# Weights of layers 2 to 4 turned on VectorE from 32-column blocks, and the first gates in a new order

## The chip, the cores and the metric

The kernel runs on one core of a Trainium2 chip. The metric is the device time of one execution in microseconds (us); shown is the median of the runs. Beside it there is one profiled execution with a trace. The engines are named as the profile names them: PE is TensorE (PEld its weight loads), DVE is VectorE, ACT is ScalarE, POOL is GpSimd, and SP is SyncE, which here only issues DMA transfers. A small q behind a name (SPq) is the engine's sequencer.

## The reference

Sixteen graphs of 1024 nodes with 128 features each. `x` is (16, 1024, 128), `adj` is (16, 1024, 1024) with entries 0 and 1. Two networks run one after the other, each on the layer norm of its input and with a residual.

```python
# first network: four layers of a gated graph network, h = relu(layernorm(x))
for i in range(4):
    hw = h @ weight[i]
    m = einsum('bjn,bjd->bnd', adj, hw)            # adj transposed
    gx, gh = m @ w_ih[i].T + b_ih[i], h @ w_hh[i].T + b_hh[i]
    r, z = sigmoid(xr + hr), sigmoid(xz + hz)      # thirds of gx and gh
    n = tanh(xn + r * hn)
    h = (1 - z) * n + z * h
x = x + h * mask
# second network: four layers of a graph convolution, h = relu(layernorm(x))
for i in range(4):
    h = relu(adj @ (h @ W[i]) + b[i])
    h = gamma[i] * (h - mean) * rsqrt(var + 1e-5) + beta[i]   # over all graphs and nodes
x = x + h
```

## The kernel before

The work is laid out by features across nodes: a hidden state is a tile of 128 features by 1024 nodes, in two halves of 512. The kernel uses `exact_path`; `general_path` stands behind a flag for other inputs and is not run here.

**First network.** Two graphs go at once, as two streams, `sa` (even graphs, A) and `sb` (odd graphs, B). A half step (`half_step(one, two)`, L1090) does the gates of stream `two` on ScalarE and VectorE while TensorE does the aggregation of stream `one`. An aggregation (`aggregate_rows`, L518) takes the features as a high and a low part (`hw[0]`, `hw[1]`) and one rounded row block of the adjacency after the other: four products of 128x512 for each of eight rows. `products` (L992) then makes the four gate sums of a half with six full f32 products. `w_mT` holds weight and w_ih multiplied together, so that `m` doesn't need its own weight product; `join_layer` (L484) makes it out of turned weights.

The order of all engines in this part is written out by hand (`tc.manual_schedule`): each engine runs its instructions as the program text lists them. An `agenda` (`at`, `due`) puts extra work at named places of a half step.

Each half of a new state goes out to DRAM and comes back with other strides (`half_out` or `turned_half` turn it in 32x32 blocks on VectorE, `exchange_out` L603 writes it, `exchange_in` L609 reads it with four transfers); all of these are issued by SP. What comes back is copied into the high part by ScalarE (`high`, L932, L937) and into the low part by VectorE (`low`, L939, L944).

**Start.** Before the loop of half steps, the first layer of graphs 0 and 1 is written out by hand (L1154 to L1282). TensorE turns the weights of layer 0 with transposes (`turn_hh`, `turn_ih`), ScalarE copies them out of PSUM, idle transposes (L1158) fill the wait for x. `first_rows` loads row blocks of the adjacency, `first_round` rounds them on GpSimd or ScalarE. Looks and glances (`first_look` on VectorE, `first_glance` on ScalarE) scan rows for values that are not exact. The order of the layer's end for A and the begin for B is:

```python
            exchange_in(out0, half_of(sa.y, 0))
            sa.candidate(1)
            ...
            out1 = turned_half(sa.new, sa.y, 1, "h0_1")
            exchange_in(out1, half_of(sa.y, 1))
```

The weights of layers 1 to 3 (in the program's count, which starts at 0; layers 2 to 4 in the title) are loaded by `load_layer` with one transfer each and turned by TensorE as well, at gaps of the aggregation. That is 21 transposes of 128x128, with copies on ScalarE.

**Second network.** Sixteen graphs times four layers of aggregation and product, ordered by the tile framework. **Tail.** After the last layer each graph's 1024 nodes are scaled (L1656 to L1662, tile `bn`), turned back by TensorE (L1667, `pt_o`), added to x by VectorE (L1669) and stored by SP (L1671 by pieces, L1673 for a whole graph); `whole` (L1508) says which.

Of the kernel before, what the change touches and what calls it, by code (L numbers as in the profile page):

```python
# [8 lines left out]
F32 = mybir.dt.float32  # L9
# [332 lines left out]
def exact_path(  # L342
# [115 lines left out]
    def load_layer(i):  # L458

        for src, nm in ((g_w_hh, "hh"), (g_w_ih, "ih")):  # L460
            wn = half_tile(f"wn_{nm}{i}").bitcast(F32)[:, : 3 * C].rearrange("p (g c) -> p g c", c=C)
            nc.sync.dma_start(wn, src[i].rearrange("(g p) c -> p g c", p=P))
            wns[nm, i] = wn
# [10 lines left out]
    def turn_ih(prep, w_g, i):  # L474
# [4 lines left out]
        nc.tensor.transpose(pt[:, 3 * P :], w_g[:, i, :], ident)  # L479
        both = prep.tile([P, 4 * C], F32, tag="w_both", name=f"w_both{i}", bufs=1)  # L480
# [50 lines left out]
    with ExitStack() as st:  # L531
# [138 lines left out]
        def norm_scale(nt, k0, k1):  # L670
            norm_invert(nt, k0, k1)
            rs, ms = (t[:, k0:k1, 0] for t in nt[2:])
            nc.vector.scalar_tensor_tensor(ms, nt[1][:, k0:k1, 0], -1.0, rs, ALU.mult, ALU.mult)
# [71 lines left out]
        class Stream:  # L745
# [231 lines left out]

            def open_reset(self):
                nc.tensor.matmul(self.opened[0], w_hhT[:, 0, :C], self.hT[:, :HALF], start=True, stop=False)

# [11 lines left out]
            def products(self, hf):  # L992
# [18 lines left out]
                if self.opened:  # L1011
                    part(pz, w_hhT, 1, hin, True, False)
# [77 lines left out]
        def half_step(one, two, gated=None, halfway=None, rest=None):  # L1090
# [32 lines left out]
            one.low(1)  # L1123
            two.candidate(1)
# [15 lines left out]
            if halfway:  # L1140
                halfway()
            one.agg_step(1)
            if rest:
                rest()
# [6 lines left out]
        with tc.manual_schedule(engines=every):  # L1151
# [8 lines left out]
            idle(20)  # L1160
# [3 lines left out]
            for k0, eng in ((0, nc.sync), (BH, nc.scalar)):  # L1164
                x0_d = x[0].rearrange("(k p) c -> p k c", p=P)[:, k0 : k0 + BH, :]
                eng.dma_start(x0[:, k0 : k0 + BH, :], x0_d)
            small_in = load_small(prep)
            load_layer(0)
            w_g = flat("w_g")[:, :L, :]
# [6 lines left out]
            first_rows(0, range(NB), raw0)  # L1176
            x1 = load_x(1, nc.sync)
            halves = [[half_tile(f"early{j}_{k}").bitcast(F32) for k in range(2)] for j in range(3)]
# [10 lines left out]
            sa.sums(range(4, 5))  # L1189
# [3 lines left out]
            turn_ih(prep, w_g, 0)  # L1193
            sa.centred_high(0)
            turn_half(sa.y, "in0", h0, 0, AF.Relu)
            sa.sums(range(5, 7))
            join_layer(0)
            pt = acc("g_xn", "pt_idle1")
            idle(6)
            sa.centred_low(0)  # L1200
            sa.sums(range(7, NB))
# [3 lines left out]
            sa.centred_high(1)  # L1205
            sa.centred_low(1)
            for j in range(4):
                sa.rows[j] = first_round(0, j, raw0[j], nc.gpsimd)
            sa.hT = h0
            sa.agg_rows(range(1))  # L1210
            sa.open_gates()
            sa.agg_rows(range(1, 4))
            sa.open_reset()
            for j in range(2):
# [3 lines left out]
            first_look(0, 2, raw0[2])  # L1218
            sa.agg_rows(range(4, 6))
            for j, eng in ((6, nc.scalar), (7, nc.gpsimd)):  # L1220
                sa.rows[j] = first_round(0, j, raw0[j], eng)
            turn_half(sa.y, "in0", h0, 1, AF.Relu)
            turn_small(*small_in)
            sa.agg_rows(range(6, NB))

            sb.sums(range(NB))
            sb.rows[0] = first_round(1, 0, raw1[0], nc.scalar)
            norm_root(sb.norm, 0, NB)
            norm_scale(sb.norm, 0, NB)
            first_look(0, 3, raw0[3])  # L1230
            first_rows(1, range(4, NB), quarters)
            for j in range(1, NB):
                sb.rows[j] = first_round(1, j, raw1[j], nc.gpsimd)

            load_layer(1)
            nc.sync.dma_start(w_g[:, 1:, :], w_d[:, 1:, :])
            nc.gpsimd.dma_start(w_c, c_w.rearrange("l c d -> c l d"))
            sb.hT, sb.across = h1, True

            def half_of(t, hf):  # L1240
                return t[:, hf * HALF : (hf + 1) * HALF]

            def beside(hf):
                sb.normed(range(hf * BH, (hf + 1) * BH))
                sb.split_high(hf)
                sb.split_low(hf)
# [6 lines left out]
            sa.products(0)  # L1253
            sa.reset_gate(0)
            sa.update_gate(0)
            beside(0)
            in0 = turned_half(sb.y, h1, 0, "in1")
            exchange_in(in0, half_of(h1, 0))
            sa.candidate(0)
            sa.less(0)  # L1260
            sa.scaled()
            beside(1)
            sa.mixed(0)
            out0 = turned_half(sa.new, sa.y, 0, "h0_1")
            in1 = turned_half(sb.y, h1, 1, "in1")
            sa.products(1)
            sa.reset_gate(1)
            for b, j, ts in ((0, 4, raw0), (0, 5, raw0), (1, 2, raw1), (0, 6, raw0)):
                first_glance(b, j, ts[j])
            exchange_in(in1, half_of(h1, 1))  # L1270
            exchange_in(out0, half_of(sa.y, 0))
            sa.candidate(1)
            sa.update_gate(1)
# [6 lines left out]
            sb.agg_rows(range(6))  # L1280
            turn_hh(1)
            sb.agg_rows(range(6, NB))  # L1282

            def looks():
                turn_ih(prep, w_g, 1)
# [3 lines left out]
            def later_layers():  # L1289
                for b, j, ts in ((0, 7, raw0), (1, 3, raw1)):  # L1290
                    first_glance(b, j, ts[j])
                for i in range(2, L):
                    load_layer(i)
# [5 lines left out]
            def both(i):  # L1299
                turn_hh(i)  # L1300
                turn_ih(prep, w_g, i)

            def ahead(i):
                join_layer(i)
                if i == 2:
# [420 lines left out]
```

## Time and profile before

| | us |
|---|---|
| median of 3 runs | 1757.21 |
| lowest and highest | 1756.29, 1757.41 |
| the profiled execution | 1755.79 |
| its span, first to last instruction | 1754.0 |
| TensorE busy | 1739.1 |
| VectorE busy | 1321.0 |
| ScalarE busy | 1156.3 |
| GpSimd busy | 389.5 |

The mean granted clock of TensorE is 0.998 of full speed. Matmuls overlap in the profile and their ends are modelled, so the distances of their starts are the better measure of what one costs. A timeline line has the start in us, the time that a merged group covers, the engine, the line of the program, the operation, out<-in, the shape and the count, and in brackets the idle time before it with what ended it. A line of the windows has the stretch, its length, the busy time of PE, PEld, DVE, ACT and POOL (with counts), the granted clock, the DMA engines' busy share and GB/s.

### The profile page before, as it was taken

The numbers are of one execution on the slowest core, as the hardware profiler recorded it, in microseconds if no ns is written. First come the engines' busy times: TensorE is split into PE (matmuls) and PEld (weight loads), VectorE is DVE, ScalarE is ACT, GpSimd is POOL, SyncE is SP. The second block draws the span as 40 slices with busy tenths as digits, with TensorE's granted clock in tenths as the row PEclk, the third lists the DMA queues.
The fourth block names the chain that finished last, engine by engine and source line by source line (L and its number), as shares of the span: only waits on it lengthen the run. The fifth ranks groups of instructions, "written<-read, shape, count | busy, mean of one in ns | idle before, by whom it ended". The sixth has DMA issues, their size and how long they took to land. (4 is left out here: it accounts for less than half of the span.)

```text
span 1754.0 us, 22125 instructions
## 1 busy us (share of the span) xinstructions
PE 1739.1 (99%) x6654; PEld 1181.4 (67%) x6654; DVE 1321.0 (75%) x2375; ACT 1156.3 (66%) x1823; POOL 389.5 (22%) x435
## 2 busy tenths in 40 slices
PE   9999999999999999999999999999999999999997
PEld 6665656565656565656565656577778888888885
DVE  6778887887887787888788787677776666666665
ACT  7467556657557566665756654467787778769875
POOL 4314223232341331431422324121100000000000
PEclk9999999999999999999999999999999999999999
DMA  8458379368557756846836836898966767757666
GB/s 290 132 139 273 103 161 295 115 176 248 171 151 209 210 153 180 255 122 177 274 104 175 282 112 175 276 311 302 314 230 233 242 239 243 260 203 270 219 240 255
DMA packets 302817, 373.40 MB, mean 213 GB/s; under 512 B 24428, under 2 KB 189072, under 8 KB 302688
## 3 DMA queue, kind: packets, MB, share of 16 engines
q1 hardware_dynamic: 291136, 334.06, 60.7%
q0 software_dynamic: 11024, 37.58, 6.7%
q8 instruction: 54, 0.88, 0.2%
q14 instruction: 75, 0.61, 0.1%
q10 hardware_dynamic: 528, 0.26, 0.0%
HBM read 271.14 MB, written 100.67 MB: 212 GB/s over the span
## 5 line engine op out<-in xcount | busy, mean ns | idle before, releaser
L522 PE MATMUL pm<-row,ghw 128*128 128x512 f32 x2048 | 503.8, 403 | 0.0
L522 PEld LDWEIGHTS pm<-row,ghw 128*128 128x128 f32 x2048 | 384.2, 188 | 105.9 <-issue 23.9
L522 PE MATMUL pc_m<-wide,chw 128*128 128x512 f32 x1024 | 245.3, 395 | 0.0
L522 PEld LDWEIGHTS pc_m<-wide,chw 128*128 128x128 f32 x1024 | 190.5, 188 | 42.6 <-issue 4.3
L967 ACT COPY m<-pm 128x512 f32<-128x512 f32 x128 | 68.7, 589 | 228.1 <-PE pm L522 228.1
L586 POOL CAST row<-stage 128x1024 fp32r<-128x1024 f32 x112 | 127.6, 1144 | 343.7 <-DMA stage<-in_adj_dram 293.6
L522 PE MATMUL pc_g_r<-wide,chw 128*128 128x512 f32 x464 | 187.3, 404 | 0.0
L522 PE MATMUL pc_g_z<-wide,chw 128*128 128x512 f32 x464 | 181.0, 390 | 0.0
L1032 DVE SCALAR_TENSOR_TENSOR r<-g_hn,vecs,r 128x512 f32<-128x512 f32 x128 | 93.4, 730 | 107.9 <-ACT r L1031 58.3
L632 POOL CAST pair<-row 128x1024 bf16<-128x1024 f32 x128 | 165.6, 1343 | 31.9 <-DVE adjT L638 31.9
L1036 ACT ACTIVATE r<-r,vecs 128x512 f32<-128x512 f32 x128 | 92.3, 721 | 115.2 <-DVE r L1033 113.0
L1372 DVE CAST wide<-block 128x1024 fp32r<-128x1024 bf16 x160 | 109.9, 693 | 62.7 <-PE pc_m L522 32.8
L1372 DVE CAST wide<-packed 128x1024 fp32r<-128x1024 bf16 x160 | 108.9, 688 | 60.3 <-PE pc_g_z L522 45.1
L1370 ACT CAST wide<-packed 128x1024 fp32r<-128x1024 bf16 x96 | 100.9, 1052 | 47.1 <-PE pc_m L522 26.9
L1009 PE MATMUL g_r<-m,w_mT 128*128 128x512 f32 x256 | 130.8, 592 | 0.2 <-ACT m L967 0.2
L1009 PE MATMUL g_xn<-m,w_mT 128*128 128x512 f32 x256 | 130.7, 592 | 0.0
L1009 PE MATMUL g_z<-m,w_mT 128*128 128x512 f32 x256 | 130.7, 592 | 0.0
L1434 DVE BATCH_NORM_STATS2 stats<-feat 128x6 f32<-128x512 f32 x129 | 85.8, 684 | 56.1 <-ACT feat L1425 35.2
L1031 ACT ACTIVATE r<-g_r,brz 128x512 f32<-128x512 f32 x128 | 88.0, 688 | 58.7 <-PE g_r L1009 58.2
L1370 ACT CAST wide<-block 128x1024 fp32r<-128x1024 bf16 x96 | 100.8, 1051 | 39.0 <-PE pc_g_z L522 21.5
L1053 DVE TENSOR_TENSOR h<-h,z 128x512 f32<-128x512 f32 x128 | 96.0, 750 | 15.7 <-ACT z L1040 4.3
L1049 DVE TENSOR_TENSOR h<-h,r 128x512 f32<-128x512 f32 x96 | 70.5, 734 | 49.0 <-ACT r L1036 48.6
(208 smaller groups left out, 2900.7 us busy)
## 6 DMA issues: line engine op xcount, KB each, us to landing
block<-adjT_d SPq DMA_DIRECT2D x256, 256.0 KB, 4.7
packed<-adjT_d SPq DMA_DIRECT2D x256, 256.0 KB, 5.6
stage<-in_adj_dram SPq DMA_DIRECT2D x120, 512.0 KB, 5.6
adjT_d<-adjT SPq DMA_DIRECT2D x64, 512.0 KB, 7.2
cross_h<-t_h SPq DMA_DIRECT2D x94, 256.0 KB, 2.1
n_h<-cross_h SPq DMA_DIRECT2D x376, 64.0 KB, 2.0
xmid_d<-x POOLq DMA_DIRECT2D x16, 512.0 KB, 3.8
x<-in_x_dram SPq DMA_DIRECT2D x15, 512.0 KB, 4.3
```

The source lines that it names most:

```text
L522: nc.tensor.matmul(pm[hf], hw[s][:, j * P : (j + 1) * P], rows[j][:, hf * HALF : (hf + 1) * HALF], start=(j == 0 and s == 0), stop=(j == N ...
L586: nc.gpsimd.tensor_copy(t, stage[j % 4])
L632: nc.gpsimd.tensor_copy(halves[:, :, o], rows[4 * o + j].bitcast(F32))
L1009: nc.tensor.matmul(po, wT[:, i, g * C : (g + 1) * C], rhs, start=start, stop=stop)
L1031: nc.scalar.activation(r, pr, AF.Sigmoid, bias=brz[:, 3 * i : 3 * i + 1])
L1032: nc.vector.scalar_tensor_tensor(r, phn, b_hn(i), r, ALU.add, ALU.mult)
L1036: nc.scalar.activation(self.r, self.r, AF.Tanh, bias=b_in(self.i))
L1049: nc.vector.tensor_sub(ho, hin, self.r)
L1053: nc.vector.tensor_mul(ho, ho, self.z)
L1370: nc.scalar.copy(r, t)
L1372: nc.vector.tensor_copy(r, t)
L1434: nc.vector.bn_stats(stats[:, b * NH + hf + k, :], dst)
```

## The change

**Weights of layers 1 to 3.** `load_blocks` brings each weight in 32-column blocks: four transfers for w_hh, four for w_ih (32 partitions x 12 x 32 values each) and four for the weight (32 x 4 x 32), all with contiguous pieces of 32 values (128 bytes), into `w_mT` and a free zone of the tile `w_g`. `turn_blocks` turns them with two block transposes on VectorE. The transposes on TensorE and the copies on ScalarE for these layers are dropped; `join_layer` stays. Layer 1's transfers are issued between the two exchanges of A's halves, layers 2 and 3's at the place `load` of the half steps 4 and 5.

**First gates.** Sixteen idle transposes in place of 20, and none of the later six. x0's second half goes by SP behind the first row; graph 1's x goes ahead of row 7. The first join stands behind row 0 of the aggregation, `g_hn` ahead of it. `h0`'s second half is turned and copied before row 4 is cast. Two products of half 1 (`open_second`) and the update gate's (`open_update`) are opened inside the aggregation; the four others of half 1 (`second_products`) follow the first half's at once. B's norm is done in one piece (`sums_at_once`) and its split in blocks of two (`split_blocks`). B's row 0 is rounded on GpSimd, row 7 of A half on ScalarE and half on GpSimd; more glances are done after the first half step.

**Tail.** Graph 2 is scaled by GpSimd; graphs 2, 3 and 4 are loaded and stored by halves.

```diff
+            def blocks_in(dst, src):
+                rows = src.rearrange("(b j) c -> j b c", j=32)
+                for a in range(4):
+                    part = slice(a * 32, (a + 1) * 32)
+                    nc.sync.dma_start(dst[part, :].rearrange("j (b i) -> j b i", i=32), rows[:, :, part])
+            def load_blocks(i):
+                blocks_in(w_mT[:, i, :], g_w_hh[i])
+                blocks_in(zone[:, : 3 * C], g_w_ih[i])
+                blocks_in(zone[:, 3 * C :], g_weight[i])
+            def turn_blocks(i):
+                nc.vector.transpose(w_hhT[:, i, :], w_mT[:, i, :])
+                both = w_g[:, :4, :].rearrange("p k c -> p (k c)") if i < 3 else cross_tile("w_both3")
+                nc.vector.transpose(both, zone)
+                turned[i] = both[:, 3 * C :], both[:, : 3 * C]
...
-            idle(20)
+            idle(16)
...
+            load_x0(0)
             small_in = load_small(prep)
             load_layer(0)
...
-            first_rows(0, range(NB), raw0)
+            first_rows(0, range(1), raw0)
+            load_x0(BH)
+            first_rows(0, range(1, 7), raw0[1:])
             x1 = load_x(1, nc.sync)
+            first_rows(0, range(7, NB), raw0[7:])
...
             turn_half(sa.y, "in0", h0, 0, AF.Relu)
-            sa.sums(range(5, 7))
-            join_layer(0)
-            pt = acc("g_xn", "pt_idle1")
-            idle(6)
-            sa.centred_low(0)
-            sa.sums(range(7, NB))
+            copy_ih(prep, both0, 0)
+            sa.centred_low(0)
+            sa.sums(range(4, NB))
+            sa.hT = h0
+            for j in range(4):
+                sa.rows[j] = first_round(0, j, raw0[j], nc.gpsimd)
+            sa.open_gates()
+            sa.agg_rows(range(1))
+            join_layer(0)
...
+            sa.agg_rows(range(1, 2))
+            turn_small(*small_in)
+            sa.centred_low(1)
             sa.open_reset()
+            sa.agg_rows(range(2, 4))
+            turn_half(sa.y, "in0", h0, 1, AF.Relu)
...
             sa.rows[4] = first_round(0, 4, raw0[4], nc.scalar)
             sa.rows[5] = first_round(0, 5, raw0[5], nc.gpsimd)
-            first_look(0, 2, raw0[2])
-            sa.agg_rows(range(4, 6))
...
+            sa.agg_rows(range(4, 5))
+            sa.rows[6] = first_round(0, 6, raw0[6], nc.scalar)
...
+            sa.agg_rows(range(5, 7))
+            sa.open_second()
+            sums_at_once(sb.xt, sb.norm)
+            sa.agg_rows(range(7, NB))
+            sa.open_update()
...
             sa.products(0)
+            sa.second_products()
             sa.reset_gate(0)
             sa.update_gate(0)
-            beside(0)
+            sb.split_blocks(0)
+            sb.split_blocks(2)
             in0 = turned_half(sb.y, h1, 0, "in1")
+            sb.split_blocks(4)
+            sb.split_blocks(6)
+            in1 = turned_half(sb.y, h1, 1, "in1")
             exchange_in(in0, half_of(h1, 0))
+            exchange_in(in1, half_of(h1, 1))
             sa.candidate(0)
...
+            first_glance(0, 4, raw0[4])
+            sa.update_gate(1)
+            first_glance(0, 5, raw0[5])
             exchange_in(out0, half_of(sa.y, 0))
+            load_blocks(1)
             sa.candidate(1)
...
             out1 = turned_half(sa.new, sa.y, 1, "h0_1")
             exchange_in(out1, half_of(sa.y, 1))
...
-            sb.agg_rows(range(6))
-            turn_hh(1)
-            sb.agg_rows(range(6, NB))
+            sb.agg_rows(range(NB))
...
-                for b, j, ts in ((0, 7, raw0), (1, 3, raw1)):
+                for b, j, ts in ((0, 6, raw0), (0, 7, raw0), (1, 2, raw1), (1, 3, raw1)):
                     first_glance(b, j, ts[j])
-                for i in range(2, L):
-                    load_layer(i)
...
+            at(3, "turned", lambda: turn_blocks(1))
+            at(3, "join", lambda: join_layer(1))
+            for i in range(2, L):
+                at(i + 2, "load", lambda i=i: load_blocks(i))
+                at(i + 2, "gap", lambda i=i: turn_blocks(i))
+                at(i + 3, "join", lambda i=i: join_layer(i))
...
     def whole(b):
-        return xo_whole[b] is not None and 1 < b < B - 1
+        return 5 < b < B - 1
...
-        if b > 1:
+        if b == 2:
+            nc.gpsimd.tensor_scalar(hT, feat[b], aff[0], aff[1], ALU.mult, ALU.add)
+        elif b > 1:
             nc.scalar.activation(hT, feat[b], AF.Identity, bias=aff[1], scale=aff[0])
```

In a half step the place `turned` stands on VectorE right behind stream `one`'s low part of half 1, and `join` on TensorE between the two halves of the aggregation.

## The prediction

> **What bounds the kernel now.** I read the page first, then the timeline of TensorE, then those of ScalarE, VectorE, GpSimd and the SP queue over the first 80 us, then the table of windows over the last 30 us.
>
> ```profile
> PE 1739.1 (99%) x6654; PEld 1181.4 (67%) x6654; DVE 1321.0 (75%) x2375; ACT 1156.3 (66%) x1823; POOL 389.5 (22%) x435
> ```
>
> TensorE is covered from 2.4 us to 1724 us, so only three things count: instructions taken off TensorE, new waits of TensorE, and the last 30 us, where it has no work to speak of. The change touches the first 130 us and the last 30 us alone.
>
> ```profile
> 9.69 1.18 PE L522 MATMUL pm<-row,ghw 128*128 128x512 f32 x4
> ...
> 28.49 6.05 PE L522 MATMUL pm<-row,ghw 128*128 128x512 f32 x24
> ...
> 47.84 3.90 PE L522 MATMUL pm<-row,ghw 128*128 128x512 f32 x16
> 51.58 0.81 PE L487 MATMUL pt_wm<-w_both 128*128 128x384 f32 x2
> 51.93 4.14 PE L522 MATMUL pm<-row,ghw 128*128 128x512 f32 x16
> ...
> 56.76 1.02 PE L1009 MATMUL g_r<-m,w_mT 128*128 128x512 f32 x2
> ...
> 66.20 0.49 PE L471 MATMUL pt_whh<-ident,wn_hh 128*128 128x128 f32 x3
> ```
>
> Durations overlap; the prices are the distances of the starts. A group of 16 aggregation products is 3.7 us (0.23 each, 0.92 a row), a gate product 0.86, three transposes 0.33 (66.20 to the next group at 66.53), a join of a layer 0.65.
>
> ```profile
> 13.25 1.05 ACT L559 CAST row<-first 128x1024 fp32r<-128x1024 f32 x1
> ...
> 17.69 0.60 ACT L697 ACTIVATE h_in<-pt_in 128x512 f32<-128x512 f32 x1 [0.82 <-PE pt_in L696]
> ...
> 47.52 0.62 ACT L937 CAST ghw<-y_in 128x512 fp32r<-128x512 f32 x1 [2.58 <-DMA y_in<-cross_h]
> ...
> 55.87 1.07 ACT L967 COPY m<-pm 128x512 f32<-128x512 f32 x2 [0.75 <-PE pm L522]
> ```
>
> ScalarE waits 2.58 us for stream A's second half to come back from DRAM (47.5 us). VectorE's low part ends at 48.86; TensorE wants it at 51.93, so 3.07 us are to spare.
>
> ```profile
> 39.79 1.73 SPq L613 DMA_DIRECT2D y_in<-cross_h  x4
> 41.62 0.36 SPq L606 DMA_DIRECT2D cross_h<-y_in  x1
> 43.97 1.73 SPq L613 DMA_DIRECT2D y_in<-cross_h  x4
> ```
>
> SP issues that round trip without a gap: out at 41.62, back from 43.97 on. One issue takes about 0.47 us.
>
> ```profile
> 1728.00:1730.00 2.00, 1.48 (x12) 1.17 (x12) 1.54 (x4) 2.00 (x3) 0.00 (x0) 1.00 0.85 321
> 1730.00:1732.00 2.00, 1.92 (x17) 1.45 (x14) 2.00 (x4) 2.00 (x3) 0.00 (x0) 1.00 0.50 200
> 1732.00:1734.00 2.00, 1.96 (x16) 1.67 (x16) 2.00 (x4) 2.00 (x2) 0.00 (x0) 1.00 1.01 408
> ...
> 1746.00:1748.00 2.00, 0.00 (x0) 0.00 (x0) 0.08 (x1) 0.00 (x0) 0.00 (x0) 0.89 1.04 401
> ```
>
> The last two columns are the DMA share and GB/s. From 1732 us the stores fill the DMA engines, so the tail ends when they do; in the four us before, 1.3 us of DMA time are unused.
>
> **The change part by part.**
>
> *First aggregation (to 28.49).* The chain x0, sums, root, `centred`, `pt_in`, `h_in` stays: its VectorE part (4.24 to 7.62) is unchanged, the fifth block's sums only filled the wait for the root. Before, `pt_in` waited at 7.83 for ScalarE's copy of `pt_whh`, and `h_in` came after the copy `w_both`. With four idle transposes less (0.21 each) the first goes 0.85 earlier, and the second is moved behind. I get: `pt_in` done 8.0, high part to 8.3, `h_in` to 8.8, `g_hn` on TensorE at 8.85, 0.84 before the old 9.69. From there to stream B's aggregation TensorE issues: `g_hn` 0.86, eight rows 7.36, the join 0.65 (it stood ahead of 9.69), the small transposes 0.38, two early products of half 0 1.72, `pt_in` 0.43, two early ones of half 1 1.72, three products 2.58, four of half 1 3.44: 19.1, to 28.0. But a wait is added. `turn_half(..., 1)` now stands ahead of row 4's cast in ScalarE's order. TensorE gets to `pt_in` half 1 at 15.3 and to row 4 at 15.7; ScalarE copies `h_in` at 15.9, and only then casts row 4 (1.05, as at 13.25): row 4 is there at 17.5. Behind that wait stands everything of TensorE: 1.8 us. Aggregation of B begins at 29.8 (before 28.49): +1.3.
>
> *To the join of layer 1 (51.58).* Taken away: three transposes inside B's aggregation (0.33), four ahead of A's (0.43 with three more), and of the waits of 0.5 us at B's first products (36.65 to 38.90, ScalarE late with `m` after glances and a weight copy) about a half: 1.0 in all. TensorE is at the join at about 51.7, nearly where it was.
>
> *The twelve block transfers of layer 1.* They stand on SP between A's first half coming back and its second half going out. The SP chain: ScalarE does B's eight blocks and four casts (4 x 1.16) ahead of A's tanh, so tanh is at 31.8, half 0 is turned at 35.5; B's two round trips hold SP to 37.4; half 0 out 37.4, back 39.7 to 41.5. Then 12 x 0.47 = 5.6 us. Half 1 is turned on VectorE at 40.9, but goes out at 47.2 instead of 41.6, is issued back from 49.4 and lands at 53.3 to 54 instead of 47.5. So the landing is 6.1 us late (5.1 if SP did everything else as before).
> Do the bytes come along? There is no row for 128-byte pieces. Nearest: x of stream B, 1024 pieces of 512 bytes, lands 1.72 us behind a row of adj (GpSimd's cast at 17.19, VectorE's sums at 18.91), 27 ns a piece on each of 16 engines. 3584 pieces are 224 an engine, 6.0 us, about the issue time. Below, the bytes alone at the rate of the rows (1.28 us for 512 KB) would be 1.1 us, and the issue still 5.6. The Trainium skill ("DMA: Bandwidth & Descriptors", Specifications) speaks against this change: under 512 bytes the engine does a read-modify-write, and full rate is lost. Taken as twice the time of a piece (an estimate) that is 12 us, the landing 6 us later still and the sum +10. I take the row, and keep both ends.
>
> *Who waits for it.* ScalarE's high part is in order ahead of B's glances, tanh and update gate, so all of that moves. VectorE turns both blocks after the low part: a 128x512 STREAM_TRANSPOSE is 0.71 and 0.63 from start to start, with 384 columns about 0.55: 1.25 in all. The join on TensorE waits for them: 53.7 + 0.1 + 0.6 + 0.05 + 0.7 + 1.25 = 56.4, a wait of 4.7 us (the delays alone, 6.1 + 1.25 less the 3.07 to spare, give 4.3). Then the join 0.65 and four rows 3.7. ScalarE, after tanh and gate, has five glances instead of two (three of 1.17, two halves of 0.76: 5.0 us), then the copy `w_mT` 0.45, then `m` 0.6. From the landing that is 0.1 + 0.55 + 1.5 (glances beside) + 1.3 (tanh, gate) + 5.0 + 0.45 + 0.6 = 9.5: `m` at 63.1, and the product that stood at 56.76 starts at about 62.8 to 63.2: +6.1 to +6.4. One thing more: the wait of 4.7 us is long enough for the clock. The last matmul ended at 1744.4 and the granted clock was 0.89 over 1746 to 1748 and 0.50 after, so it falls about 3.2 us after the last work; at the start it took 4.3 us of work (2.42 to 6.74) to get the full clock. Four rows at half clock would be up to 2 us more, but they have 1.6 us until `m` comes: 0 to 2, I take 0.2. At this place: +6.3.
>
> *Layers 2 and 3.* Removed: seven transposes at 66.20, three at 71.26, four at 75.24: 14 x 0.108 = 1.5 off TensorE, all on the path. Their 12 transfers each stand on SP behind the `n_h` reads; SP was idle from 60.70 to 64.64, so A's first half goes out up to 2 us late, but its reads wait for the second half (70.1). In the next step x and the turned rows' stores follow them, and `cross_h` (84.43) comes some 3 us late; again the second half (89.88) is the later. VectorE's turns, 1.25 each, fall where it idles 3.35 us (before 78.53) and 1.41 (before 96.81). Cost nothing; without that cover 1.25 each.
>
> *Edits with one answer: nothing.* Sums of x1 at once (5 small instructions for 8 aggregates, needed at 27, done at 22); B's row 0 on GpSimd (1.3 us more there; its last row, 31, is wanted at 36); row 7 behind x1 (there at 19.1, wanted at 22.0); the second half of x0 behind a row (sums done 10.7; ScalarE asks at 11.9).
>
> *Tail.* Batch 2's affine goes to GpSimd: it must be done by 1727.9, begins at 1724.6; the nearest row, a cast of the same size, is 1.0 to 1.3 us, and up to 3.3 is free. ScalarE's next ones come 1.13 earlier, VectorE's gap of 0.44 ahead of 1729.25 goes, and batches 2 to 4 are stored by halves: the first at 1729.4 and not 1730.6. DMA then fills from 1729 and not 1732: of the 1.3 unused about 1.0 comes back, less 0.2 for halves of 2 KB rows. -0.8 (0 to -1.3).
>
> **Sum:** +6.3 - 1.5 - 0.8 = +4.0 on this execution's own 1755.8 (span 1754.0 and 1.8 around it): 1759.8. The execution lies 1.4 under the median of the runs, 1757.2, so 1761.2.
>
> **The rivals.**
> *B, the delay does not reach TensorE.* If the second half goes out less than 2 us late (SP issuing the short transfers in a third of 0.47 us each, or TensorE itself so late that the order doesn't matter), the +6.3 shrinks to what the head gives. At a landing under 49.5 us the sum is zero; with none it is 0 - 1.5 - 0.8 = -2.3, 1754.9. If row 4's cast then isn't waited for either, -4.1, 1753.1. For it: the order is clearly written to take work off TensorE, and 3 us were to spare. Against it: no issue of SP in the first 80 us is shorter than 0.3 us.
> *C, the short pieces are dear.* At 54 ns a piece the round trip stands 6 us longer behind them in the same queue: +10, 1767; the clock is lost for longer too. For it the skill's rule; against it 27 ns for 512-byte pieces.
>
> **How the numbers follow.** Likeliest, as worked out, 0.62: +2.5 to +7, 1759.7 to 1764.2. B 0.20, C 0.18. About 0.2% (3.5 us) is what a measurement of this kernel can tell from no change. The likeliest case lies astride it: 0.42 slower, 0.20 within. B gives 0.12 within, 0.08 faster; C slower. Together 0.08, 0.32, 0.60. The range 1754.5 to 1767 leaves out the faster part of B and half of C.
>
> **What would show it.** Right: TensorE idle about 1.8 us before row 4 near 16 us; `m` or the join late near 52 to 63 us, with SP's `cross_h` of A's second half at 47 and ScalarE waiting past 52 for its landing; no transposes after 10 us; DMA share near 1 from 1729 on. Wrong: a join at 51 to 52 us without idle time (B), or block transfers landing at 4 us apart (C). Wrong altogether: a difference that arises between 130 and 1700 us, where the instructions are the same.

## The result, and the profile after

| | before | after |
|---|---|---|
| median, us | 1757.12 (7 runs, 1756.23 to 1757.52) | 1762.60 (7 runs, 1760.69 to 1764.67) |
| profiled execution, us | 1755.79 | 1763.04 |
| its span, us | 1754.0 | 1761.3 |

The ratio of after to before is 1.0031, interval [1.0021, 1.0041]: slower by 5.5 us. The prediction said 1761.2, 4 us slower.

The first line is from the page: TensorE has 31 instructions fewer and is as busy as before. The lines under the dots are the timeline of TensorE.

```profile
PE 1739.2 (99%) x6623; PEld 1179.1 (67%) x6623; DVE 1316.1 (75%) x2380; ACT 1151.4 (65%) x1817; POOL 391.7 (22%) x441
...
17.90 3.02 PE L528 MATMUL pm<-row,ghw 128*128 128x512 f32 x12 [1.62 <-ACT row L565]
...
30.05 7.83 PE L528 MATMUL pm<-row,ghw 128*128 128x512 f32 x32
...
48.29 4.23 PE L528 MATMUL pm<-row,ghw 128*128 128x512 f32 x16
56.20 1.65 PE L493 MATMUL pt_wm<-w_g 128*128 128x384 f32 x2 [3.67 <-DVE w_g L1312]
57.07 6.19 PE L528 MATMUL pm<-row,ghw 128*128 128x512 f32 x16
63.09 1.02 PE L1065 MATMUL g_r<-h,w_hhT 128*128 128x512 f32 x2
63.95 1.02 PE L1065 MATMUL g_r<-m,w_mT 128*128 128x512 f32 x2
```

Three things are to be seen. Row 4 is waited for (1.62 us, behind ScalarE's cast), and B's aggregation begins at 30.05 and not 28.49. The join of layer 1 waits 3.67 us for the turned weights. And the sixteen products behind it take 6.02 us (57.07 to 63.09), where the same sixteen took 3.97 before (51.93 to 55.90). The product on `m` that stood at 56.76 stands at 63.95, 7.2 us later. The sixteen of before end ahead of this line of its timeline:

```profile
55.90 1.02 PE L1009 MATMUL g_r<-h,w_hhT 128*128 128x512 f32 x2
```

The SP queue's timeline says why the join waits, those of ScalarE and VectorE say how the delay is handed on:

```profile
40.22 1.73 SPq L619 DMA_DIRECT2D y_in<-cross_h  x4
41.99 1.97 SPq L1302 DMA_DIRECT2D w_mT<-in_L_gnn_w_hh_dram  x4
44.00 2.14 SPq L1302 DMA_DIRECT2D w_g<-in_L_gnn_w_ih_dram  x4
46.19 1.89 SPq L1302 DMA_DIRECT2D w_g<-in_L_gnn_weight_dram  x4
48.19 0.36 SPq L612 DMA_DIRECT2D cross_h<-y_in  x1
50.38 1.73 SPq L619 DMA_DIRECT2D y_in<-cross_h  x4
...
53.72 0.62 ACT L956 CAST ghw<-y_in 128x512 fp32r<-128x512 f32 x1 [7.58 <-DMA y_in<-cross_h]
...
54.37 0.69 DVE L963 TENSOR_TENSOR ghw<-y_in,ghw 128x512 fp32r<-128x512 f32 x1 [5.75 <-ACT ghw L956]
54.98 0.57 DVE L1310 STREAM_TRANSPOSE w_hhT<-w_mT 128x384 f32<-128x384 f32 x1
55.47 0.67 DVE L1312 STREAM_TRANSPOSE w_g<-w_g 128x512 f32<-128x512 f32 x1
```

A's second half is turned on VectorE by 41.5, but SP issues twelve transfers from 41.99 to 48.08 first, so it goes out at 48.19 and lands at 53.7 (before: 41.62 and 47.5). ScalarE, VectorE's low part, the two turns and the join follow one another from there.

The slow products are explained by the windows, whose last three columns are the granted clock, the DMA share and GB/s:

```profile
52.00:54.00 2.00, 0.52 (x3) 0.10 (x1) 0.00 (x0) 0.28 (x1) 0.00 (x0) 1.00 0.68 225
54.00:56.00 2.00, 0.00 (x0) 0.00 (x0) 1.63 (x3) 1.97 (x6) 0.00 (x0) 0.66 0.00 0
56.00:58.00 2.00, 1.80 (x3) 1.17 (x4) 1.64 (x4) 1.97 (x5) 0.00 (x0) 0.50 0.00 0
58.00:60.00 2.00, 2.00 (x6) 1.54 (x5) 1.97 (x3) 1.94 (x5) 1.36 (x2) 0.50 0.00 0
60.00:62.00 2.00, 2.00 (x7) 1.53 (x7) 2.00 (x3) 1.97 (x5) 1.38 (x2) 0.64 0.54 189
```

TensorE's work ends at 52.5, the clock is halved inside 54 to 56 us (a share of 0.66 over two microseconds puts it at 54.6), and it is whole again only inside 60 to 62 (0.64 puts it at 61.4).

### The profile page after: what moved, and what is told of

It is laid out like the page before. It is cut to its first block, busy times and chain, and to the rows that moved or that the text cites. A ratio compares the mean times of both kernels' runs of the same rounds, so it can differ in the third digit from the quotient of the medians.

```text
span 1761.3 us, 22122 instructions
## 1 busy us (share of the span) xinstructions
PE 1739.2 (99%) x6623; PEld 1179.1 (67%) x6623; DVE 1316.1 (75%) x2380; ACT 1151.4 (65%) x1817; POOL 391.7 (22%) x441
## 5 line engine op out<-in xcount | busy, mean ns | idle before, releaser
L1104 DVE TENSOR_TENSOR h<-h,r 128x512 f32<-128x512 f32 x96 | 70.4, 734 | 53.7 <-ACT r L1091 53.7
```

Of the source, the lines that this page charges most:

```text
L1104: nc.vector.tensor_sub(ho, hin, self.r)
```

## The experiments

Theory: the twelve transfers of layer 1 are in the wrong place of SP's queue, and everything else is small. Rivals: the short pieces are dear in themselves; the new order of the first gates is slow; the slow clock, not the wait, is the loss. Each of the twelve times is a median beside runs of the kernel before on the same chip; the timelines are of one profiled execution each. "The product on `m`" is the first product on the first half's `m` behind layer 1's join: 56.76 before, 63.95 after.

**1. The transfers earlier.** They are issued behind the last rows of graph 1.

```diff
             first_rows(1, range(4, NB), quarters)
+            load_blocks(1)
...
             exchange_in(out0, half_of(sa.y, 0))
-            load_blocks(1)
```

> Layer 1's twelve block transfers are issued right behind the last rows of graph 1 (SP is idle from 24.9 to 31.3 us there) and no longer between the round trips of A's two halves; all else is the changed kernel's. Theory (SP's issue time delays A's second half): half 1 goes out near 41.6 and not 48.2, lands near 47.5 and not 53.7, TensorE's wait of 3.7 us at the join is gone, the four rows behind it run at full clock, and the product on m stands near 57.8 and not 63.95 (-6.1). Total near 1756.5 against 1762.6, ratio to the kernel before 0.9990 to 1.0005. Rival 1 (the short pieces themselves hold the DMA engines or their data come late): the rows of graph 1 or B's first round trip come late instead, and less than half of the 6 us is won. Rival 2 (the new order of the first gates costs the time, the transfers only fill a wait): the join stays at 55 us or later, total 1761 or more.

Measured: 1759.19 (21 runs, 1756.81 to 1763.78), ratio 1.0013 [1.0006, 1.0020]. From the timelines of the SP queue and of TensorE, and the windows:

```profile
24.78 2.34 SPq L1297 DMA_DIRECT2D w_mT<-in_L_gnn_w_hh_dram  x4
27.17 4.88 SPq L1297 DMA_DIRECT2D w_g<-in_L_gnn_w_ih_dram  x4
32.09 3.26 SPq L1297 DMA_DIRECT2D w_g<-in_L_gnn_weight_dram  x4
35.45 0.85 SPq L612 DMA_DIRECT2D cross_in<-h_in  x2
...
41.06 2.05 PE L1065 MATMUL g_r<-h_in,w_hhT 128*128 128x512 f32 x2 [3.12 <-DMA h_in<-cross_in]
...
40.00:42.00 2.00, 0.94 (x1) 0.50 (x2) 1.51 (x3) 0.00 (x0) 0.00 (x0) 0.60 0.47 134
46.00:48.00 2.00, 2.00 (x4) 0.75 (x3) 0.92 (x2) 0.87 (x4) 0.00 (x0) 0.69 0.43 158
```

The wait at the join is gone, and a little over half of the loss with it. But a new wait of 3.1 us stands at B's first products: the twelve issues took 10.6 us (24.78 to 35.4, 0.88 each and not 0.51) while the rows ahead of them were still in flight (whether these are the reason was not tested), and B's write, which had begun at 31.25, began at 35.45. In that wait the clock fell as well: by the shares 0.60 and 0.69 it is halved from 40.4 to 47.2. TensorE, at work again from 41.06, lost 3.1 us by it, half of those 6.2 and as much as by the wait itself. In the profiled execution the product on `m` is at 63.33, so there nearly all was lost again. The runs spread over 7 us, and the clock goes with the spread: the ten with a mean clock of 0.998 or more have a median of 1758.33, the other eleven of 1760.11. Rival 1 is right in kind: SP's idle stretch was no free place.

**2. Row 4 first.** ScalarE's cast of row 4 is put ahead of the copy of `h0`'s second half.

```diff
+            sa.rows[4] = first_round(0, 4, raw0[4], nc.scalar)
             turn_half(sa.y, "in0", h0, 1, AF.Relu)
             for j in range(2):
                 first_look(0, j, raw0[j])
-            sa.rows[4] = first_round(0, 4, raw0[4], nc.scalar)
```

> ScalarE casts row 4 of graph 0 ahead of the copy of the second half of h0; nothing else is moved. Theory: TensorE's wait of 1.6 us before row 4 goes, B's aggregation begins near 28.5 and not 30.05; the gates of A, the round trips and so the transfers of blocks come 1 to 1.5 us earlier too, so the product on m stands near 62.5 to 63 and not 63.95, total -1 to -1.5 (near 1761.3). Rival: from B's split on, ScalarE and VectorE set the pace and not TensorE; then A's second half lands at 53.7 as it did, TensorE waits 1.5 us longer at the join, and the total stays.

Measured: 1762.40, ratio 1.0030 [1.0017, 1.0042]. TensorE's timeline:

```profile
16.59 3.12 PE L528 MATMUL pm<-row,ghw 128*128 128x512 f32 x12
...
56.27 1.65 PE L493 MATMUL pt_wm<-w_g 128*128 128x384 f32 x2 [4.62 <-DVE w_g L1312]
...
64.02 1.02 PE L1065 MATMUL g_r<-m,w_mT 128*128 128x512 f32 x2
```

The wait for row 4 is gone, the wait at the join is 1 us longer, and the product on `m` is where it was. The theory for this run fell and its rival held: SP, held by B's round trip, writes A's first half at 37.66 (before this edit 37.95), so TensorE's gain at 16 us never reaches the queue that sets the end.

**3. Idle transposes in the wait.** They keep TensorE at work until just before the join.

```diff
+            def warm(n):
+                pt = tmp("pt_warm")
+                for k in range(n):
+                    nc.tensor.transpose(pt[:, k % 4 * P : (k % 4 + 1) * P], ident, ident)
...
-            at(3, "join", lambda: join_layer(1))
+            at(3, "join", lambda: (warm(30), join_layer(1)))
```

> Thirty idle transposes (0.11 us each, 3.3 us) stand on TensorE ahead of layer 1's join, in the wait for it; they change no result. It prices the clock term alone. Theory: the sixteen products behind the join take 3.7 us at full clock and not 6.0 at half clock; ScalarE then sets the next product instead of TensorE (five glances and the copy end at 62.2), so only 0.9 of the 2.3 us is won: product on m near 63.0 and not 63.95, total -0.9 against the changed kernel. Rival: the products are slow for another reason (rows or features read late): they still take 6 us and nothing is won.

Measured: 1762.78 (1759.97 to 1764.75), ratio 1.0032 [1.0020, 1.0043]. TensorE's timeline:

```profile
52.97 3.44 PE L1359 MATMUL pt_warm<-ident 128*128 128x128 f32 x30
58.12 0.88 PE L493 MATMUL pt_wm<-w_g 128*128 128x384 f32 x2 [1.72 <-DVE w_g L1312]
58.55 4.14 PE L528 MATMUL pm<-row,ghw 128*128 128x512 f32 x16
62.53 1.02 PE L1065 MATMUL g_r<-h,w_hhT 128*128 128x512 f32 x2
64.56 1.12 PE L1065 MATMUL g_r<-m,w_mT 128*128 128x512 f32 x2 [1.01 <-ACT m L986]
```

The sixteen products take 3.98 us (58.55 to 62.53), so the clock is what made them slow. Behind them the product now waits 1.0 us for ScalarE, which had five glances and the copies to do. In this execution A's second half landed at 55.55, 1.8 later than in the changed kernel's; from landing to product on `m` it is 9.0 us here and 10.2 there, so the slow clock cost 1.2 on the path, as far as one execution of each can tell. The total doesn't show that: the runs spread over 4.8 us.

**4. The tail alone**, put into the kernel before.

```diff
     def whole(b):
-        return xo_whole[b] is not None and 1 < b < B - 1
+        return 5 < b < B - 1
...
-        if b > 1:
+        if b == 2:
+            nc.gpsimd.tensor_scalar(hT, feat[b], aff[0], aff[1], ALU.mult, ALU.add)
+        elif b > 1:
```

> The kernel before with the tail's part of the change alone: graph 2 scaled by GpSimd, graphs 2 to 4 loaded and stored by halves. Theory: the last store ends 0.5 us earlier (as between the two traces) to 0.8 (as forecast), ratio 0.9995 to 0.9997. Rival: the stores fill the DMA engines anyway, and the halves of 2 KB rows cost what the earlier start brings: no difference or slower by up to 0.5 us.

Measured: 1756.14 against 1757.09, ratio 0.9993 [0.9984, 1.0001]: too small for the runs to show, but VectorE's adds, shifted by 3.99 us against the trace of before up to the one that stood at 1728.11, are shifted by 3.47 from the next on (1729.25): 0.52 won, as in the changed kernel (7.93 to 7.40). The 3.99 itself is of another kind. TensorE's waits of 1140 to 1200 us in this trace are

```profile
PE pc_m L522 <- ACT chw L1451: 1.0, 1, 1.0
PE pc_m L522 <- DVE chw L1452: 0.5, 1, 0.5
...
1162.00:1164.00 2.00, 2.00 (x6) 1.59 (x5) 0.69 (x1) 0.50 (x1) 2.00 (x4) 0.50 1.07 384
```

and the trace of before has no wait there, though both kernels have the same instructions in that stretch. The window below them shows what came of two waits so short: the granted clock is 0.84 over 1160 to 1162, 0.50 over the next two microseconds and 0.81 to 1166, so it was halved for 3.4 us, and TensorE lost 1.7. Waits and clock together are 3.2 of the 3.99. The profiled execution (1759.5) was the slowest of this kernel's 13. So there are slips of 1 to 4 us in the middle of the program that belong to the execution and not to the edit.

**5. Layer 1 in the old way**, everything else changed: three plain transfers, seven transposes on TensorE, no blocks.

```diff
             first_rows(1, range(4, NB), quarters)
+            load_layer(1)
+            nc.sync.dma_start(zone[:, 3 * C :], g_weight[1])
...
-            load_blocks(1)
...
-            sb.agg_rows(range(NB))
+            sb.agg_rows(range(6))
+            turn_hh(1)
+            sb.agg_rows(range(6, NB))
...
+            def turn_one():
+                pt = tmp("pt_wih1")
+                for g in range(3):
+                    nc.tensor.transpose(pt[:, g * P : (g + 1) * P], wns["ih", 1][:, g, :], ident)
+                nc.tensor.transpose(pt[:, 3 * P :], zone[:, 3 * C :], ident)
+                both = w_g[:, :4, :].rearrange("p k c -> p (k c)")
+                nc.scalar.copy(both, pt)
+                turned[1] = both[:, 3 * C :], both[:, : 3 * C]
...
             def looks():
+                turn_one()
...
-            at(3, "turned", lambda: turn_blocks(1))
```

> Layer 1's weights alone go the old way: three plain transfers behind the last rows of graph 1, seven transposes on TensorE with their two copies on ScalarE; layers 2 and 3 stay in blocks, the new order of the first gates and the tail stay. Theory (the twelve transfers between the round trips are the loss): A's second half lands near 47.6, no wait at the join, the product on m near 58.6 (57.8 and 0.8 for the transposes) and not 63.95; total near 1757.3 (-5.3), ratio to the kernel before about 1.000. Rival (the new order of the first gates is itself slower than the old one): the product on m stays above 61, total above 1760.

Measured: 1756.87 against 1757.65, ratio 0.9994 [0.9986, 1.0003]. ScalarE's and TensorE's timelines:

```profile
48.69 0.62 ACT L956 CAST ghw<-y_in 128x512 fp32r<-128x512 f32 x1 [2.04 <-DMA y_in<-cross_h]
...
53.32 0.81 PE L493 MATMUL pt_wm<-w_g 128*128 128x384 f32 x2
...
58.50 1.02 PE L1065 MATMUL g_r<-m,w_mT 128*128 128x512 f32 x2
```

No wait at the join, the product on `m` at 58.50 (58.6 was expected). Its interval and the changed kernel's don't touch: the way of layer 1's weights is the whole loss, and the new order of the first gates with the blocks of layers 2 and 3 and the tail is no slower than before. The new order alone is not free: it still has the wait of 1.6 us for row 4, and the product on `m` is 1.7 later than before (58.50 against 56.76). Layers 2 and 3 and the tail win that back.

**6 and 7. The transfers on GpSimd's queue, with short and with long pieces.** First only the queue is changed; then the twelve transfers also read contiguous runs.

```diff
-            def blocks_in(dst, src):
+            def blocks_in(dst, src, eng=nc.sync):
                 rows = src.rearrange("(b j) c -> j b c", j=32)
+                if eng is nc.gpsimd:                                       # second kernel alone
+                    plain = src.rearrange("(p q) c -> p (q c)", p=P)       # second kernel alone
                 for a in range(4):
                     part = slice(a * 32, (a + 1) * 32)
-                    nc.sync.dma_start(dst[part, :].rearrange("j (b i) -> j b i", i=32), rows[:, :, part])
+                    if eng is nc.gpsimd:                                   # second kernel alone
+                        eng.dma_start(dst[part, :], plain[part, :])        # second kernel alone
+                        continue                                           # second kernel alone
+                    eng.dma_start(dst[part, :].rearrange("j (b i) -> j b i", i=32), rows[:, :, part])
...
             def load_blocks(i):
+                eng = nc.gpsimd if i == 1 else nc.sync
```

> The same twelve block transfers of layer 1, issued on GpSimd's queue and not SP's; GpSimd issues them when its casts end, near 32 us. Theory (SP's issue slots are the loss, not the bytes): B's and A's round trips on SP stand as if the blocks were not there, half 1 lands near 47.6, no wait at the join, product on m near 57.8, total near 1756.5 (-6.1). Rival 1 (the short pieces cost the DMA engines or their descriptors cost GpSimd so much that they land after 50 us): TensorE waits at the join again, by landing less 50; at 4 us or more of it nothing is won. Rival 2 (they collide with B's round trip, as behind the rows of graph 1, where 3.1 us of wait arose at B's first products): a wait on h_in of 1 to 3 us and a total of 1758 to 1760.

> As the run with layer 1's blocks on GpSimd's queue (1759.3), but each of the twelve transfers reads contiguous runs (1536 or 512 bytes a partition) in place of 128-byte pieces: as many transfers, partitions and bytes. Layer 1's weights are then not turned rightly, so this kernel doesn't compute the reference. It separates short pieces from mere traffic beside B's round trip. Theory (traffic and queue slots): TensorE still waits 2 to 2.7 us on h_in, the total stays within 1 us of 1759.3. Rival (short pieces take the DMA engines' time): h_in lands about 2.0 us after its issue and not 3.5, the wait is gone, total near 1757.

Measured: short pieces 1759.30 against 1757.65, ratio 1.0010 [1.0002, 1.0018]; long ones 1756.92 against 1757.23, ratio 1.0001 [0.9993, 1.0009]. TensorE's first product of B and the landing time of the reads ahead of it (last column of the DMA view's issues, 31 to 45 us), first the short pieces, then the long ones:

```profile
40.14 1.10 PE L1065 MATMUL g_r<-h_in,w_hhT 128*128 128x512 f32 x2 [2.43 <-DMA h_in<-cross_in]
...
h_in<-cross_in SPq DMA_DIRECT2D x8, 64.0 KB, 3.5
```

```profile
39.39 1.10 PE L1065 MATMUL g_r<-h_in,w_hhT 128*128 128x512 f32 x2 [1.06 <-DMA h_in<-cross_in]
...
h_in<-cross_in SPq DMA_DIRECT2D x8, 64.0 KB, 2.9
```

In the changed kernel these reads land 2.0 us after their issue. So leaving the place ahead of A's second half was worth 3 to 4 us of the 5.5, but beside B's round trip the same bytes are in the way again. Short pieces cost more there than long ones (wait 2.4 against 1.1; the product on `m` is at 59.37 against 58.61, although B's aggregation began 0.6 earlier), though not all: traffic alone takes 1.1. The clock was whole in both executions. Of the 13 runs with short pieces six have a mean clock of 0.997 and a median of 1760.03, the seven at 0.998 a median of 1758.17: 3.4 us at half clock, as in the next experiments, would be 0.001 of the mean, so the clock probably fell in those six. No trace shows it. Neither expectation of the second kernel held cleanly; it lies between, and the two intervals overlap.

**8 to 11. Combinations.** Blocks on GpSimd's queue with row 4 first; this with two glances moved; layer 1 in the old way with both; and the twelve transfers behind B's first write with both:

```diff
+            for b, j, ts in ((0, 6, raw0), (1, 2, raw1)):
+                first_glance(b, j, ts[j])
             sb.agg_rows(range(NB))
...
-                for b, j, ts in ((0, 6, raw0), (0, 7, raw0), (1, 2, raw1), (1, 3, raw1)):
+                for b, j, ts in ((0, 7, raw0), (1, 3, raw1)):
...
-            load_blocks(1)                                   # fourth kernel alone, as below
...
-            at(3, "turned", lambda: turn_blocks(1))
-            at(3, "join", lambda: join_layer(1))
+            at(3, "beside1", lambda: load_blocks(1))
+            at(3, "outs", lambda: turn_blocks(1))
+            at(4, "start", lambda: join_layer(1))
```

> Blocks of layer 1 on GpSimd's queue and row 4 cast ahead of the copy of h0's second half. Row 4 alone brought nothing (1762.4 against 1762.6), because the landing of A's second half set the end. Theory: with that landing out of the way the 1.6 us count, as far as ScalarE's five glances allow (m at about 57 by ScalarE): product on m near 57.0, total 0.8 under the kernel with the blocks on GpSimd's queue alone. Rival: ScalarE or VectorE sets the pace in A's first gates, and again nothing comes of it.

> As the one before, and two of the five glances (row 6 of graph 0, row 2 of graph 1) ahead of the landing of A's second half, where ScalarE waits. Theory: m is no longer late on ScalarE; product on m near 56.2, total near 1754.9, ratio to the kernel before 0.9988. Rival: ScalarE had no room ahead of the landing any more, the high part of the second half comes later and the product on m with it (57 or later): equal to the one before or worse.

> Layer 1's weights in the old way (as in the run that gave 1756.9), row 4 cast ahead of the copy of h0's second half, two of the five glances moved ahead of the landing of A's second half. Theory: nothing else stands behind row 4's wait now, so its 1.6 us reach the product on m: 57.0 and not 58.5, total near 1755.4, ratio to the kernel before 0.9988. Rival: B's first round trip (written at 31 us) sets B's first products, as in two of the runs with row 4 alone and with GpSimd's queue: a wait of 0.7 to 1.5 us on h_in there, total 1756.2 or more.

> Layer 1's twelve block transfers on SP behind the write of B's first new half (from about 46.7 us, where SP would wait for the second), turned on VectorE behind that second half, joined behind the aggregation; row 4 and two glances as in the kernel sent beside it. Theory: the transfers cost only where a round trip stands behind them in the queue or beside them on the DMA engines; here only B's second write does, which is ready at 53. No wait at the join, product on m near 56.5 (0.8 less than with transposes), total near 1754.7, ratio 0.9984. Rival: B's second half goes out late behind them (after 53.5), n_h comes back late and TensorE waits in the next half step by 1 us or more; total above 1756.

Measured: 1758.28, 1758.01, 1758.92 and 1759.02; ratios 1.0006 [0.9998, 1.0015], 1.0003 [0.9995, 1.0012], 1.0010 [1.0001, 1.0018] and 1.0009 [1.0000, 1.0017]. In none did the product on `m` come to where the theory had it. The first total is 1.0 under experiment 6, as its theory said, but the two intervals overlap. In the first two the waits on `h_in` (2.7 and 2.5 us) stay, and the clock falls. TensorE's timeline of the first:

```profile
39.46 1.47 PE L1065 MATMUL g_r<-h_in,w_hhT 128*128 128x512 f32 x2 [2.74 <-DMA h_in<-cross_in]
40.73 1.92 PE L1065 MATMUL g_r<-m,w_mT 128*128 128x512 f32 x2
...
60.37 1.02 PE L1065 MATMUL g_r<-m,w_mT 128*128 128x512 f32 x2
```

Row 4 did bring B's first product 0.7 earlier than in experiment 6 (39.46 against 40.14). But the group behind it takes 1.92 where 1.02 is usual: the clock is halved from 40.0 to 43.5. From B's first product to the product on `m` it is 20.9 us here and 19.2 in experiment 6, so 1.7 went to the clock. In the last two the moved glances are themselves the fault, as TensorE's timeline shows:

```profile
40.65 2.07 PE L1065 MATMUL g_r<-m,w_mT 128*128 128x512 f32 x2 [2.81 <-ACT m L986]
```

(the kernel with layer 1 in the old way; 2.20 in the one with late transfers). They had been put ahead of B's copies of `m` in ScalarE's order, not into the stretch in which ScalarE waits for A's second half. Behind both waits the clock was halved for 3.4 us too.

**12. Late transfers, the glances in their place.** As the last of these, but:

```diff
-            for b, j, ts in ((0, 6, raw0), (1, 2, raw1)):
-                first_glance(b, j, ts[j])
             sb.agg_rows(range(NB))
...
+            at(3, "mid", lambda: [first_glance(b, j, ts[j]) for b, j, ts in ((0, 6, raw0), (1, 2, raw1))])
```

> As the kernel with layer 1's transfers behind the write of B's first half, but with the two glances where ScalarE waits for the landing of A's second half (behind the high part of the first), and not ahead of B's copies of m, where they made TensorE wait 2.2 to 2.8 us in the two runs before. Theory: that wait goes, only h_in's 0.7 is left, and three causes are out of the way at once (SP's issue time ahead of A's second half, row 4's wait, the transposes of layer 1): product on m near 56.5 to 57.3, total near 1755, ratio to the kernel before 0.998 to 0.9995. Rival: the late return of B's first half, or the transfers ahead of B's second write, set the pace: product on m at 58 or later, total no better than the 1756.9 of the kernel with layer 1 in the old way.

Measured: 1756.77 against 1758.11, ratio 0.9993 [0.9984, 1.0001]. TensorE's timeline:

```profile
37.01 1.10 PE L1065 MATMUL g_r<-h_in,w_hhT 128*128 128x512 f32 x2 [0.62 <-DMA h_in<-cross_in]
...
56.77 0.91 PE L493 MATMUL pt_wm<-w_g 128*128 128x384 f32 x2 [1.77 <-DVE w_g L1312]
...
58.38 1.02 PE L1065 MATMUL g_r<-m,w_mT 128*128 128x512 f32 x2
```

The wait on `m` is gone and the clock stays whole, but the join, although it stands behind the aggregation now, waits 1.77 us: B's first write goes out at 48.08, the twelve issues end at 54.46. The product on `m` is at 58.38, where the rival put it. This kernel and the one with layer 1 in the old way are 6 us better than the change and about 0.07% under the kernel before, which the intervals don't tell from no change. No version was shown to beat both.

## Why the prediction was right, and where it was off

- **Start, +1.3.** Right in cause and size, a wait of 1.62 (1.8 forecast), B's aggregation +1.56. But it was no term of the sum: the second experiment took the wait away and the end stayed. The path had already passed to SP's queue.
- **The twelve transfers, 5.6 us of SP, landing at 53.3 to 54.** Held: 6.2 us from the first of them to A's write, 0.52 each and not 0.47, landing at 53.7. Two small misses met in that landing: the reads were issued at 50.38 and not 49.4, and came back in 3.3 us (3.6 before) where the forecast left 3.9 to 4.6. The fifth experiment shows that this is the whole loss.
- **The join at 56.4.** Held: 56.20. TensorE could have been there at 52.0 (48.29 and the 3.74 that sixteen products take up to the join in the trace of before), so it came 4.2 late, 4.7 forecast.
- **The clock, 0 to 2, taken as 0.2.** This is the term that was mis-sized. At half clock the join took 0.87 (57.07 less 56.20) and not 0.35, the products 6.02 and not 3.97: 2.6 us, where "up to 2" counted the rows alone. The 1.6 us of cover were right: ScalarE was free at 62.18 (its copy of `w_mT` at 61.72 took 0.46), and at full clock the products would have ended at 60.5 (56.20 and 0.35 and 3.97). What was over, 0.9, fell on the path: ScalarE waited 0.88 for TensorE and began to copy `m` at 63.06, so TensorE was the later one. The forecast had that copy done by 63.1 and named ScalarE as the one that sets it.
- **Product on `m`, +6.1 to +6.4.** Measured +7.2. The 0.9 between them is the clock on the path; without it (third experiment) the chain is 1.2 shorter, and then ScalarE is late, as the working said.
- **Layers 2 and 3, -1.5.** The shift of ScalarE's `m` copies against before falls from +7.19 at the end of that half step to +6.1 once layer 3 is joined too, and is +5.88 from 147 to 280 us: -1.3. The transfers and turns of these layers cost no wait of TensorE.
- **Tail, -0.8.** -0.53, inside the 0 to -1.3 given. The gap of VectorE closed; filling the DMA engines earlier brought nothing beyond it.
- **The sum.** +7.2 - 1.3 - 0.5 = +5.4 for +4.0 forecast, and the medians differ by 5.5. The profiled execution is 7.25 above that of before: the other 2 are slips at 292 us (+1.2, behind waits of ScalarE of 1.5 for `n_h` and 1.1 for a load of stage rows), near 313 (+0.2, behind one of 2.9 for such a load) and near 1165 us (+0.7). The run with row 4 first has the same instructions there and a shift of 5.9 throughout, so they are not the change's. What makes such a load late in one execution stays open; that the clock can then add to it, experiment 4 shows.
- **Rival B (the delay does not reach TensorE)** fell: the twelve issues of 0.47 to 0.54 us each did delay A's write, and the landing at 53.7 is far beyond 49.5. **Rival C (the short pieces are dear, the landing 6 us later still)** fell for this kernel: the three kinds of transfers landed 1.8 to 2.2 us (medians) after their issue, so the bytes kept up with SP's issues; and four issues of 16 KB took 1.89 us, four of 48 KB 1.97 and 2.14, so the bytes hardly set the time of an issue. Its rule was weighed at 54 ns a piece, the nearest row at 27. The windows give less than both, by the last two columns (DMA share and GB/s) of a stretch that moves nothing but blocks, beside one that moves nothing but rows:

```profile
24.00:26.00 2.00, 2.00 (x6) 0.97 (x6) 0.46 (x1) 1.97 (x3) 1.28 (x3) 1.00 1.03 412
...
44.00:46.00 2.00, 2.00 (x6) 0.92 (x5) 1.90 (x4) 1.48 (x3) 0.00 (x0) 1.00 0.63 101
```

101 GB/s are 789 pieces of 128 bytes in a microsecond; at 0.63 of 16 engines that is 12.8 ns a piece, or 160 GB/s for full engines where rows get 400. So the Trainium skill's rule ("DMA: Bandwidth & Descriptors", Specifications: under 512 bytes full rate is lost) agrees with this trace in kind; the engines were merely not the limit, SP's issue rate was. Where short pieces were put beside another round trip (experiment 6, against long ones in 7), the rule did show.

## What to carry to other kernels

Work taken off the busiest engine is paid for on the queue that now carries it: count the transfers, multiply by the time of one issue, and ask whose round trip stands behind them in that queue. A wait of a few microseconds in front of TensorE can cost more than itself, because the work behind it may run at half clock (1.7 to 3.1 us lost here); price both, and look at the granted clock behind every wait, also of an experiment. And a wait removed upstream (row 4) is worth nothing until the later one is gone: find the last one first.

## What the hardware did that was not expected

- After 3.7 us without a matmul TensorE worked at half clock for 5.2 us (from 56.2; 0.50 granted to 60 us, and 0.64 over 60 to 62 puts the return at 61.4) and lost 2.6 us by it. The Trainium skill ("TensorE: Matmul & The Clock Gate", Part 1: The HAM clock gate) has the array at half rate until about 4 us of sustained work; here it was longer, in experiment 1 longer still (6.2, from 41.06 to 47.2), and in experiment 10 shorter (3.3, from 40.65 to 44.0).
- The length of a wait didn't decide alone. Behind 2.43 us (experiment 6) the clock stayed whole, behind 2.20 (experiment 11) and behind 1.0 and 0.5 close together (experiment 4) it fell. By the windows the half clock lasted 6.8 us in the change and in experiments 1 and 2, and half of that, 3.4 us, in 4 and 8 to 11. Outside experiment 4 it began 2.1 to 3.3 us after TensorE's last work, in 8 and 11 when TensorE was already at work again.
- Twelve issues of short-piece transfers took SP 6.1 us with no row loads in flight (the change), and 10.6 us behind row loads (experiment 1).
- Two kernels with the same instructions over a thousand microseconds can differ by 1 to 4 us there in one execution (2.1 in the change, 3.7 in experiment 4); a difference of two profiled executions is read by its offsets along the time, not by its end.
